# Layer 0 norms applied to the rows as they lie, and all clamps on GpSimd, in a bidirectional minGRU and ternary FFN kernel

## The chip, the cores and the metric

The kernel runs on one core of a Trainium2 chip. The metric is the device time of one execution in microseconds; of the kernel before there are three runs. A profiled execution gives a trace of every engine: TensorE (PE, with its weight loads as PEld), VectorE (DVE), ScalarE (ACT), GpSimd (POOL) and the sequencer that issues most transfers (SP).

## The reference, cut to what matters

`x` is 8 sequences of 512 tokens of 512 features. Each goes through a stack of four minGRU layers forwards and, reversed, backwards, with the same weights; the two results are fused by one linear layer and added to `x`, and a ternary feed-forward block follows.

```python
z = sigmoid(x @ Wz.T + bz);  h_tilde = tanh(x @ Wh.T + bh)
a = clip(1.0 - z, 1e-8, 1.0 - 1e-8)
h_t = a_t * h_(t-1) + z_t * h_tilde_t          # linear scan over the tokens
h = layernorm(h_new + (h if i > 0 else 0)) * gamma + beta    # over the features of a token
```

Here `Wz` is `Wh` and `bz` is `bh`, so a layer needs one matrix product. The forget factors `a` are clipped. A layer's norm needs mean and variance over the 512 features of each token.

## The kernel before, in words

Activations lie turned, with features on the 128 partitions (4 chunks of 128) and the 512 tokens along the free dimension, so that a scan over tokens is one VectorE instruction for a chunk. Sequences are worked in four pairs (0,1), (2,3), (4,5), (6,7); a state is a key `(b, d)` of sequence and direction. Layer 0 is shared by the two directions: one product for a chunk, two scans (`first_layer`, L523). For layers 1 to 3, `layer` (L579) runs the four states of the pair in turn.

Work is laid down in slots (`slot`, L464). A slot holds the four matmuls of one output chunk (`gates`, L482, or a chunk of `first_layer`), ScalarE's three activations (`factors`, L501: a, t, z), then on VectorE clamp, product, scan and residual, and between them pieces of earlier norms that two lists hand out: `turns` and `backs`. The slots are only a count, `now[0]`, at the time of writing: an item is taken when its due count is reached. The order on each engine is fixed by this program; engines meet by semaphores. Pools can hold an engine up: `ps_t` has 2 buffers (pt), `ps_u` 4, `tok` 10, `z` 16.

A norm (`norm`, L340) works by token tile. A turn transposes 128 tokens of the four chunks into a PSUM tile pt (L316), VectorE takes the statistics (`stats`, L168: bn_stats, bn_aggr, variance plus eps, minus mean), GpSimd the power -0.5 (L178), ScalarE writes the normalised token tile tok (L188, L189). When all four tok tiles stand, four back items transpose them to features again (pf, L325) and ScalarE writes `h * gamma + beta` chunk by chunk (L331). The norm of the last layer (`norm_last`, L354) takes only statistics, since its scale goes into the fusion; for the forward states of sequences 3, 5 and 7 ScalarE takes them in two passes over the tile (`two_passes`, L393: copy with a sum, square with a sum).

The norm of the input `x` is folded into layer 0: its weights are centred, and the product is multiplied by a tile `scale[b]` that holds each token's factor along the free dimension on all partitions. `scale_x` (L380) makes it by transposing a broadcast column on TensorE (L385) and copying it on ScalarE (L389).

The clamp of `a` is a VectorE instruction (L510) in all but the layer 0 chunks of sequences 0 and 1, where GpSimd makes it.

Layer 0 of the next pair is interleaved with the fusion of the pair before (L843 to L849): eight fusion tiles (two products, two VectorE steps L634, a store) and eight chunks; there VectorE also makes ternary weights (L193, L194), with loads and stores on SP. After that, layer 1 of the pair begins. All transfers in this stretch are issued by SP in program order.

Of the kernel before, what the change touches and what calls it, by code (L numbers as in the profile page):

```python
# [9 lines left out]
F32 = mybir.dt.float32  # L10
F32R = mybir.dt.float32r
AF = mybir.ActivationFunctionType
ALU = mybir.AluOpType
# [3 lines left out]
P = 128  # L17
LN_EPS = 1e-5
# [6 lines left out]
def kernel(  # L25
# [26 lines left out]
    nc = tc.nc  # L52
# [176 lines left out]
    with rec:  # L229
# [14 lines left out]
        class Tokens(list):  # L244
# [4 lines left out]
            def append(self, tile_):  # L249
                super().append(tile_)  # L250
                self.at = now[0] + self.lag

        def ready(at):
            if isinstance(at, Tokens):
                return len(at) == NT and at.at <= now[0]
            return at <= now[0] and held[0] < TOK

        def shares(cap):


            last = []
            for q in (turns, backs):
                some = []
                for i in range(max(2, cap)):
                    if not q or not ready(q[0][0]):
                        break
                    at, piece = q[0][:2]
                    late = (at.at if isinstance(at, Tokens) else at) + piece <= now[0]
# [71 lines left out]
        def norm(s, zs, tag, pause, pair=1):  # L340
# [10 lines left out]
            for c in range(NC_):  # L351
                queue(backs, s, toks, c // pair, back(toks, dst, c, True, f"{tag}_{c}"))

        def norm_last(s, tag):  # L354
            rsv[s] = small.tile([P, NT], F32, tag="rsv", name=f"rsv_{tag}")
            zs = [state[s][:, c, :] for c in range(NC_)]
            for t in range(NT):
                source, name = turned(zs, t, f"{tag}_{t}"), f"{tag}_{t}"
                queue(turns, s, now[0] + NC_ + 1, t, by_scalar(s, t, source, name) if s[0] > 1 and s[0] % 2 and s[1] == 0 else
                      tokens(source, None, rsv[s][:, t : t + 1], name))  # L360

        def by_scalar(s, t, source, name):
# [15 lines left out]
        rx, scale = {}, {}  # L378

        def scale_x(b):  # L380

            def go():
                pf = ps_f.tile([P, S], F32, tag="pf", name=f"pr_{b}")
                for t in range(NT):
                    nc.tensor.transpose(pf[:, ts(t, P)], rx[b][:, t : t + 1].broadcast_to([P, P]), ident)  # L385

                def last():
                    scale[b] = gp.tile([P, S], F32, tag="scale", bufs=2, name=f"scale_{b}")
                    nc.scalar.copy(scale[b], pf)  # L389
                return last  # L390
            return go
# [90 lines left out]
        def gates(h, l, o, name, scans):  # L482

            def work():
                u = ps_u.tile([P, S], F32, tag="u", name=f"u_{name}")
                for c in range(NC_):
                    nc.tensor.matmul(  # L487
                        u, lhsT=gw[l][:, c, ts(o, P)], rhs=h[:, c, :],
                        start=(c == 0), stop=(c == NC_ - 1),
                    )  # L490
                z = zp.tile([P, S], F32, tag="z", name=f"z_{name}")
                zlive[0] += 1
                a, t = factors(u, z, l, o, name)

                def end():
                    product(a, z, t)
                    scans(a, z)
                return end
            return work
# [9 lines left out]
        def clamp(engine, a):  # L509
            engine.tensor_scalar(a, a, CLAMP_HI, CLAMP_LO, ALU.min, ALU.max)  # L510

        def product(a, z, t, early=False):
            if not early:
                clamp(nc.vector, a)
            nc.vector.tensor_tensor(z, z, t, ALU.mult)  # L515

        def scan(dst, a, z, backward):
# [5 lines left out]
        def first_layer(b, lag=0):  # L523


            zf, zb = [], []

            def chunk(o):
                def work():
                    while zlive[0] + 2 > ZT:  # L530
                        slot(None, 2)
                    zlive[0] += 2
                    name = f"{b}_0_{o}"
                    u = ps_u.tile([P, S], F32, tag="u", name=f"u_{name}")
                    for c in range(NC_):
                        nc.tensor.matmul(  # L536
                            u, lhsT=gw[0][:, c, ts(o, P)], rhs=xT[b][:, c, :],
                            start=(c == 0), stop=(c == NC_ - 1),
                        )
                        if (b, o, c) in midway:  # L540
                            midway.pop((b, o, c))()

                    wait = 1 if (b, o) == (0, 0) else 0

                    def scaled():
                        z = zp.tile([P, S], F32, tag="z", name=f"z_{name}")
                        nc.vector.tensor_tensor(z, u, scale[b], ALU.mult)
                        a, t = factors(z, z, 0, o, name)

                        if b < 2:  # L550
                            stages.append((now[0], "clamps", lambda: clamp(nc.gpsimd, a)))
                        if wait:
                            for i, v in enumerate((bet, gam)):
                                nc.vector.tensor_copy(both[:, :, i, :], v.unsqueeze(2).broadcast_to([P, NC_, 64]))

                        def scans():
                            product(a, z, t, b < 2)
# [542 lines left out]
```

## Time and profile before

| | |
|---|---|
| median of 3 runs | 1714.09 us (1713.87 to 1714.39) |
| span of the profiled execution | 1711.6 us; its own time is not listed apart from this span, and the median stands 2.5 us above it |
| TensorE busy | 1701.2 us (99%) |
| VectorE busy | 1439.8 us (84%) |
| ScalarE busy | 1093.5 us (64%) |
| GpSimd busy | 222.5 us (13%) |
| granted TensorE clock | 1.000 |
| recurrent part | about 0 to 1240 us; feed-forward block behind it |

Times in the profile are microseconds from the first instruction. In a row of the timeline stand start, length, engine, line, operation, output and inputs; a bracket names how long the engine sat idle before and what ended that. Matmuls are pipelined, so a record is longer than the time that it adds: four transposes have a record of 0.60 us and the next row starts 0.43 or 0.44 us later. Records of VectorE overlap a little in the same way, and starts are the better measure. Layer 0 of the second pair lies at about 265 to 357 us, of the third at 561 to 656 us, of the fourth at 860 to 955 us. In the diff's count pairs begin with 1, so "pairs 2 to 4" are sequences 2 to 7.

### The profile page before, as it was taken

The page shows a single profiled execution, that of the slowest core. Times are in us where ns is not written, and L with a number is a line of the kernel's source. Part 1 is how long each engine was busy: PE and PEld are TensorE (multiplying, and loading weights), DVE is VectorE, ACT ScalarE, POOL GpSimd, SP SyncE. Part 2 cuts the span into 40 slices and gives each one's busy share as a digit, 9 for nine tenths or more (in the row PEclk, how much of TensorE's full clock was granted, in tenths as well). Part 3 has the DMA queues.
Part 4 walks back from the last instruction along what each step waited for, and adds up shares of the span by engine and source line. Part 5 has one row for each costly group of instructions (what it writes and reads, how often), then busy time and mean ns, then how long its engine had stood idle before and what let it go on. Part 6 is the DMA issues. An engine that isn't in the chain of part 4 may idle for free.

```text
span 1711.6 us, 19811 instructions
## 1 busy us (share of the span) xinstructions
PE 1701.2 (99%) x6440; PEld 1041.3 (61%) x6440; DVE 1439.8 (84%) x2835; ACT 1093.5 (64%) x1918; POOL 222.5 (13%) x342
## 2 busy tenths in 40 slices
PE   9999999999999999999999999999999999999999
PEld 5455554555555455555545555554688888888887
DVE  8999989889998888999888899995568768768877
ACT  6898873468886346888535688862356566666654
POOL 3111111111111111112111111110000000000000
PEclk9999999999999999999999999999999999999999
DMA  7002221150000125000012200102201101100100
GB/s 271 19 25 81 99 93 37 66 192 20 13 1 1 56 68 191 19 13 0 1 56 74 98 25 25 75 1 99 74 1 50 50 1 50 50 21 30 50 19 32
DMA packets 46599, 91.75 MB, mean 54 GB/s; under 512 B 5280, under 2 KB 5536, under 8 KB 45472
## 3 DMA queue, kind: packets, MB, share of 16 engines
q1 hardware_dynamic: 45488, 88.78, 15.2%
q10 hardware_dynamic: 1008, 1.70, 0.3%
q8 instruction: 51, 0.84, 0.2%
q14 instruction: 52, 0.43, 0.1%
HBM read 65.30 MB, written 25.17 MB: 53 GB/s over the span
## 4 chain that ended last, share of the span: by engine, by line
PE 86%; DVE 11%; ACT 2%; issue 1%; DMA 0%; POOL 0%; DVEq 0%; ACTq 0%
PE u L487 28%; PE po L939 14%; PE ph L912 14%; PE pu L624 13%; PE u L536 6%; PE pt L316 5%; PE pf L325 4%; DVE z L519 3%; DVE st L171 2%; DVE z L590 2%; DVE z L515 2%; PE py L214 1%; DVE a L510 1%; DVE mv L173 1%; ACT tok L189 0%
## 5 line engine op out<-in xcount | busy, mean ns | idle before, releaser
L487 PE MATMUL u<-xT,gw 128*128 128x512 f32 x768 | 345.5, 593 | 0.0
L487 PE MATMUL u<-h,gw 128*128 128x512 f32 x768 | 345.5, 592 | 0.0
L519 DVE TENSOR_TENSOR_SCAN z<-a,z 128x512 f32<-128x512 f32 x224 | 274.9, 1227 | 7.6
L487 PEld LDWEIGHTS u<-xT,gw 128*128 128x128 f32 x768 | 138.8, 190 | 138.7 <-issue 136.8
L487 PEld LDWEIGHTS u<-h,gw 128*128 128x128 f32 x768 | 138.6, 190 | 138.2 <-issue 138.0
L178 POOL TENSOR_TENSOR rs<-ve,mhalf 128x1 f32<-128x1 f32 x192 | 121.3, 632 | 672.7 <-DVE nmu L182 644.3
L939 PE MATMUL po<-pwq,ghi 128*128 128x512 f32 x512 | 202.8, 396 | 0.0
L939 PE MATMUL po<-pwq,glo 128*128 128x512 f32 x512 | 199.7, 390 | 0.0
L912 PE MATMUL ph<-yhi,fcq 128*128 128x512 f32 x512 | 199.7, 390 | 0.0
L504 ACT ACTIVATE a<-u,ngb 128x512 f32<-128x512 f32 x192 | 131.3, 684 | 107.0 <-PE u L487 106.3
L912 PE MATMUL ph<-ylo,fcq 128*128 128x512 f32 x512 | 199.4, 389 | 0.0
L916 ACT ACTIVATE g<-ph 128x512 f32<-128x512 f32 x128 | 76.4, 597 | 186.5 <-PE ph L912 186.5
L171 DVE BATCH_NORM_STATS2 st<-pt 128x6 f32<-128x512 f32 x244 | 168.6, 691 | 29.0 <-PE pt L316 28.8
L515 DVE TENSOR_TENSOR z<-z,t 128x512 f32<-128x512 f32 x224 | 153.5, 685 | 10.5 <-ACT z L506 10.5
L189 ACT ACTIVATE tok<-pt,nmr,rs 128x512 f32<-128x512 f32 x192 | 149.4, 778 | 6.4
L927 DVE TENSOR_TENSOR acc<-acc,g 128x512 f32<-128x512 f32 x112 | 77.3, 690 | 85.1 <-ACT g L916 84.2
L506 ACT ACTIVATE z<-u,gb 128x512 f32<-128x512 f32 x192 | 132.6, 691 | 0.0
L505 ACT ACTIVATE t<-u,gb 128x512 f32<-128x512 f32 x192 | 131.0, 682 | 0.0
L316 PEld LDWEIGHTS pt<-ident,z 128*128 128x128 f32 x640 | 78.6, 141 | 77.9 <-issue 55.5
L188 ACT ACTIVATE nmr<-nmu,rs 128x1 f32<-128x1 f32 x192 | 56.7, 295 | 106.9 <-POOL rs L178 95.5
L536 PE MATMUL u<-xT,gw 128*128 128x512 f32 x256 | 115.0, 593 | 0.8 <-DVE gw L769 0.8
L624 PE MATMUL pu<-fw,xT 128*128 128x512 f32 x256 | 115.2, 593 | 0.0
(165 smaller groups left out, 2646.3 us busy)
## 6 DMA issues: line engine op xcount, KB each, us to landing
xf<-in_x_dram SPq DMA_DIRECT2D x32, 256.0 KB, 5.5
x<-xf SPq DMA_DIRECT2D x32, 256.0 KB, 2.0
xy<-x SPq DMA_DIRECT2D x32, 256.0 KB, 4.3
xn<-in_x_dram SPq DMA_DIRECT2D x31, 256.0 KB, 4.3
out_dram<-xy SPq DMA_DIRECT2D x31, 256.0 KB, 2.0
xT<-in_xt_dram SPq DMA_DIRECT2D x7, 1024.0 KB, 7.5
fca<-in_fc_wT_dram SPq DMA_DIRECT2D x16, 256.0 KB, 2.9
pwa<-in_proj_wT_dram SPq DMA_DIRECT2D x16, 256.0 KB, 2.6
```

Of the source, the lines that this page charges most:

```text
L171: nc.vector.bn_stats(st, src)
L189: nc.scalar.activation(dst, src, AF.Identity, bias=nmr, scale=rs)
L316: nc.tensor.transpose(pt[:, ts(c, P)], zs[c][:, ts(t, P)], ident)
L487: nc.tensor.matmul(u, lhsT=gw[l][:, c, ts(o, P)], rhs=h[:, c, :], start=(c == 0), stop=(c == NC_ - 1),)
L504: nc.scalar.activation(a, u, AF.Sigmoid, bias=ngb[:, l, o : o + 1], scale=-1.0)
L506: nc.scalar.activation(z, u, AF.Sigmoid, bias=gb[:, l, o : o + 1])
L515: nc.vector.tensor_tensor(z, z, t, ALU.mult)
L519: nc.vector.tensor_tensor_scan(dst[:, d], a[:, d], z[:, d], 0.0, ALU.mult, ALU.add)
L536: nc.tensor.matmul(u, lhsT=gw[0][:, c, ts(o, P)], rhs=xT[b][:, c, :], start=(c == 0), stop=(c == NC_ - 1),)
L624: nc.tensor.matmul(pu, lhsT=hs[d][:, c, ts(t, P)], rhs=fw[:, d * NC_ + c, :], start=(c == 0), stop=(c == NC_ - 1),)
L912: nc.tensor.matmul(ph, lhsT=w, rhs=ys[b][c][i], start=(c == 0 and i == 0), stop=(c == NC_ - 1 and i == 1),)
L939: nc.tensor.matmul(po[b][t], lhsT=part[:, ts(t, P)], rhs=pwq[k // NP_][:, k % NP_, :], start=(k == 0 and i == 0), stop=(k == NF - 1 and i ...
```

## The change

For sequences 2 to 7 the norm of layer 0 is made by a new function, `norm_rows`. The turns stay: transposes into pt, statistics for each token tile, of tiles 0 and 1 by ScalarE in two passes, of tiles 2 and 3 by VectorE. Means and variances gather in a small tile pk; after the fourth tile one eps addition and one pow on GpSimd finish it. No tok tile is written and nothing is transposed back. Instead SP writes pk to DRAM as two rows of 512 numbers, and two further transfers spread each row over 128 partitions into two [128, 512] tiles. VectorE then subtracts the one from and multiplies the other into each chunk as it lies, and ScalarE applies gamma and beta to the result. These applications are due two slots after the rows were asked for.

The tile `scale[b]` of sequences 2 to 7 is spread by transfers in the same way. The last norm of the forward states of sequences 2, 4 and 6 also goes to ScalarE's two passes. Every clamp of `a` is given to GpSimd. For the first of each pair, turns and backs of layer 0 are handed out one a slot, for the second two a slot.

```diff
+        def spread(dst, i, row):
+            nc.sync.dma_start(out=dst, in_=row[i : i + 1, :].broadcast_to([P, S]))
+
+        def norm_rows(s, zs, tag, pause, pair=1):
+            rows_, at = Rows(), now[0] + pause
+            pk = small.tile([P, 2, NT], F32, tag="pk", bufs=6, name=f"pk_{tag}")
+            wide = []
+            def close():
+                nc.vector.tensor_scalar(pk[:, 1, :], pk[:, 1, :], LN_EPS, None, ALU.add)
+                nc.gpsimd.tensor_tensor(pk[:, 1, :], pk[:, 1, :], mhalf.broadcast_to([P, NT]), ALU.pow)
+                row = dram.tile([2, S], F32, tag=f"row_{tag}", name=f"row_{tag}")
+                nc.sync.dma_start(out=row.rearrange("i (t p) -> p i t", p=P), in_=pk)
+                for i in range(2):
+                    wide.append(tokp.tile([P, S], F32, tag="tok", name=f"wide{i}_{tag}"))
+                    spread(wide[i], i, row)
+                rows_.at = now[0] + 2
+            def turn(t):
+                source, name = turned(zs, t, f"{tag}_{t}"), f"{tag}_{t}"
+                def go():
+                    src = source()
...
+                    if t >= 2:
+                        st = small.tile([P, 6], F32, tag="st", name=f"st_{name}")
+                        nc.vector.bn_stats(st, src)
+                        nc.vector.bn_aggr(pk[:, :, t], st)
+                        if t == NT - 1:
+                            close()
+                        return lambda: None
+                    def last():
+                        sm, ss = (small.tile([P, 1], F32, tag=k, name=f"{k}_{name}") for k in ("sm", "ss"))
+                        mean, var = pk[:, 0, t : t + 1], pk[:, 1, t : t + 1]
+                        nc.scalar.activation(src, src, AF.Copy, accum_out=sm)
+                        nc.scalar.activation(mean, sm, AF.Copy, scale=1.0 / H)
+                        nc.scalar.activation(src, src, AF.Square, bias=mean, scale=-1.0, accum_out=ss)
+                        nc.scalar.activation(var, ss, AF.Copy, scale=1.0 / H)
+                    return last
+                return go
+            def apply(c):
+                def go():
+                    nc.vector.tensor_tensor(zs[c], zs[c], wide[0], ALU.subtract)
+                    nc.vector.tensor_tensor(zs[c], zs[c], wide[1], ALU.mult)
...
+                    def last():
...
+                        nc.scalar.activation(
+                            state[s][:, c, :], zs[c], AF.Identity,
+                            bias=bet[:, c : c + 1], scale=gam[:, c : c + 1],
+                        )
+                    return last
+                return go
+            for t in range(NT):
+                queue(turns, s, at, t // pair, turn(t))
+            for c in range(NC_):
+                queue(backs, s, rows_, c // pair, apply(c))
...
         def norm_last(s, tag):
...
-                queue(turns, s, now[0] + NC_ + 1, t, by_scalar(s, t, source, name) if s[0] > 1 and s[0] % 2 and s[1] == 0 else
+                queue(turns, s, now[0] + NC_ + 1, t, by_scalar(s, t, source, name) if s[0] > 1 and s[1] == 0 else
...
         def scale_x(b):
+            def spread_x():
+                row = dram.tile([1, S], F32, tag=f"rowx_{b}", name=f"rowx_{b}")
+                nc.sync.dma_start(out=row.rearrange("i (t p) -> p (i t)", p=P), in_=rx[b])
+                scale[b] = gp.tile([P, S], F32, tag="scale", bufs=2, name=f"scale_{b}")
+                spread(scale[b], 0, row)
+            if b > 1:
+                return spread_x
...
                 a, t = factors(u, z, l, o, name)
+                clamp(nc.gpsimd, a)
...
-        def product(a, z, t, early=False):
-            if not early:
-                clamp(nc.vector, a)
+        def product(z, t):
             nc.vector.tensor_tensor(z, z, t, ALU.mult)
...
-                        if b < 2:
-                            stages.append((now[0], "clamps", lambda: clamp(nc.gpsimd, a)))
+                        stages.append((now[0], "clamps", lambda: clamp(nc.gpsimd, a)))
...
-                                norm((b, 0), zf, f"{b}0_0", 2 if b == 1 else 1, 2 if b < 2 else 1)
+                                (norm if b < 2 else norm_rows)((b, 0), zf, f"{b}0_0", 2 if b == 1 else 1, 2 if b < 2 or b % 2 else 1)
...
-                                    norm((b, 1), zb, f"{b}1_0", 2 if b == 1 else 1, 2 if b < 2 else 1)
+                                    (norm if b < 2 else norm_rows)((b, 1), zb, f"{b}1_0", 2 if b == 1 else 1, 2 if b < 2 or b % 2 else 1)
```

More of the change, by code (lines that the diff above doesn't have):

```diff
@@ L251, in append @@
                 self.at = now[0] + self.lag
+        class Rows:
+            at = None
         def ready(at):
+            if isinstance(at, Rows):
+                return at.at is not None and at.at <= now[0]
             if isinstance(at, Tokens):
@@ L267, in shares @@
                     at, piece = q[0][:2]
-                    late = (at.at if isinstance(at, Tokens) else at) + piece <= now[0]
+                    late = (at.at if isinstance(at, (Tokens, Rows)) else at) + piece <= now[0]
                     if i >= cap and not late:
@@ L352, in norm @@
                 queue(backs, s, toks, c // pair, back(toks, dst, c, True, f"{tag}_{c}"))
+        def spread(dst, i, row):
[17 more added lines that the diff above has]
+                    src = source()
+                    if t == 0:
+                        held[0] += 2
+                    if t >= 2:
[18 more added lines that the diff above has]
+                    nc.vector.tensor_tensor(zs[c], zs[c], wide[1], ALU.mult)
+                    zlive[0] -= 1
+                    if c == NC_ - 1:
+                        held[0] -= 2
+                    def last():
+                        if s not in state:
+                            state[s] = hp.tile([P, NC_, S], F32, tag="h", name=f"h_{s[0]}{s[1]}")
+                        nc.scalar.activation(
[8 more added lines that the diff above has]
+                queue(backs, s, rows_, c // pair, apply(c))
@@ L493, in work @@
                 a, t = factors(u, z, l, o, name)
+                clamp(nc.gpsimd, a)
                 def end():
-                    product(a, z, t)
+                    product(z, t)
                     scans(a, z)
@@ L556, in scans @@
                         def scans():
-                            product(a, z, t, b < 2)
+                            product(z, t)
                             f = zp.tile([P, S], F32, tag="z", name=f"zf_{name}")
```

## The prediction

> **What bounds the kernel now.** I read the busy table first, then the windows of the stages that the change touches, then TensorE's and VectorE's rows in time through one layer 0 to layer 1 passage, and last the rows where GpSimd clamps already run.
>
> ```profile
> PE 1701.2 (99%) x6440; PEld 1041.3 (61%) x6440; DVE 1439.8 (84%) x2835; ACT 1093.5 (64%) x1918; POOL 222.5 (13%) x342
> ...
> 561.00:656.00 95.00, 95.00 (x302) 47.72 (x301) 80.09 (x148) 38.06 (x71) 11.29 (x17) 1.00 0.26 84
> 656.00:735.00 79.00, 78.76 (x291) 42.60 (x290) 73.13 (x161) 65.36 (x112) 14.30 (x23) 1.00 0.23 80
> ```
>
> In the windows the columns after the length are PE, PEld, DVE, ACT and POOL. TensorE never pauses, so only fewer matmuls or transposes can save time. But from 656 on, where layer 1 of a pair begins, VectorE is 93% busy: it is a second bound close behind.
>
> ```profile
> 690.93 0.69 DVE L171 BATCH_NORM_STATS2 st<-pt 128x6 f32<-128x512 f32 x1
> 691.66 0.18 DVE L173 BATCH_NORM_AGGREGATE mv<-st 128x2 f32<-128x6 f32 x1
> 691.95 0.15 DVE L177 TENSOR_SCALAR ve<-mv 128x1 f32<-128x1 f32 x1
> 692.02 0.14 DVE L182 TENSOR_SCALAR nmu<-mv 128x1 f32<-128x1 f32 x1
> 692.08 0.42 DVE L510 TENSOR_SCALAR a<-a 128x512 f32<-128x512 f32 x1
> 692.42 0.68 DVE L515 TENSOR_TENSOR z<-z,t 128x512 f32<-128x512 f32 x1
> 693.13 1.22 DVE L519 TENSOR_TENSOR_SCAN z<-a,z 128x512 f32<-128x512 f32 x1
> 694.39 0.69 DVE L590 TENSOR_TENSOR z<-z,h 128x512 f32<-128x512 f32 x1
> ```
>
> One VectorE slot. Records overlap, so I price by start to start: bn_stats 0.73, aggregate 0.29, each small 0.065, clamp 0.33, product 0.72, scan 1.25, residual 0.61: 4.07 us with the next start, against 4.31 us of TensorE (3.44 of matmuls and two groups of four transposes, 0.43 each).
>
> ```profile
> 635.47 3.60 PE L536 MATMUL u<-xT,gw 128*128 128x512 f32 x8
> ...
> 668.16 0.66 PE L316 MATMUL pt<-ident,z 128*128 128x128 f32 x4 [0.24 <-ACT tok L189]
> ...
> 698.81 0.60 PE L325 MATMUL pf<-ident,tok 128*128 128x128 f32 x4
> ```
>
> From the last layer 0 chunk of the pair (635.47) to the first transposes back of layer 1's first norm (698.81) TensorE takes 63.34 us, with one wait of 0.24. The second end is a hard link: those transposes need the last of four token tiles.
>
> ```profile
> 696.16 0.15 DVE L177 TENSOR_SCALAR ve<-mv 128x1 f32<-128x1 f32 x1
> ...
> 697.48 0.78 ACT L189 ACTIVATE tok<-pt,nmr,rs 128x512 f32<-128x512 f32 x1
> ```
>
> That tile ended at 698.26, 2.1 us after VectorE's eps addition and 0.55 before TensorE wanted it. VectorE can fall behind here by half a microsecond before TensorE waits.
>
> **The change, part by part.**
>
> *TensorE.* Per pair from the second on 4 x 16 transposes back and 2 x 4 of the scale go: 72 x 0.109 = 7.85 us, in all 23.5 us. With nothing else in the way the span becomes 1688.1. Of each 7.85 us, 52 transposes (5.7 us) lie between the two rows above, and 20 (2.2 us) outside.
>
> *VectorE in that stretch.* Counted in the order of instructions from the multiplication by the scale in the pair's last chunk to that eps addition. Before: 13 bn_stats, 13 aggregates, 24 small, 9 clamps, 9 products, 10 scans, 8 residuals, 5 ternary pairs (0.515 + 0.67), 4 fusion steps (0.75), 2 bias additions (0.60), the multiplication (0.65): 52.4 us. The trace has 57.2 us there, of which 4.4 are waits (1.58, 1.50, 0.92, 0.40): 56.8, so the prices hold. After: 4 bn_stats, 4 aggregates, 14 small and 9 clamps fewer (8 us less), and 14 subtractions and 14 multiplications by the spread tiles more. These read two SBUF tiles as product and residual do: 0.73 (its partner waits for it) and 0.61, 18.8 us. Sum 63.2 us.
>
> Ahead of it stand one statistic, its eps addition and two such pairs (3.8), and two fusion steps (1.5), so it starts 5.3 us after TensorE begins that chunk. With the tail of 2.1 the end cannot come before 5.3 + 63.2 + 2.1 = 70.6 us: 7.3 later than today's 63.3, although TensorE alone would need 57.6. Net of the 2.2 saved outside: **+5.1 us per pair, a floor.**
>
> *ScalarE's order.* ScalarE now takes the statistics of tiles 0 and 1 in two passes (0.58 + 0.19 + 0.20 + 0.66 + 0.19: 1.83 us each). For the norm of (b+1, forward) they stand behind the affines of two chunks that wait for VectorE, which reaches them 24.3 us into the stretch; TensorE wants the two pt buffers back at 21.5. They come free at 26.2 and 28.1, so TensorE waits and VectorE, next in need of tiles 2 and 3, idles 0.8 and 0.9. With a like knot later: +2.2 (0 to 4).
>
> *GpSimd clamps.* 216 go from VectorE (0.33 us of occupancy each) to GpSimd.
>
> ```profile
> 21.74 1.23 DVE L519 TENSOR_TENSOR_SCAN zf<-a,z 128x512 f32<-128x512 f32 x1
> 22.88 1.56 DVE L519 TENSOR_TENSOR_SCAN z<-a,z 128x512 f32<-128x512 f32 x1
> ...
> 22.13 1.24 POOL L510 TENSOR_SCALAR a<-a 128x512 f32<-128x512 f32 x1
> ```
>
> A clamp takes 0.61 alone (the shortest of 8); beside a scan it takes 1.24, and the scan behind it 1.56 instead of 1.23. So a clamp that falls among two-input operations gives its 0.33 back. The Trainium skill, "SBUF — State Buffer", section "SBUF: two separate sides", says that the two engines share a port pair by an exclusive lock for a whole instruction. By that rule a scan would be held up to 0.61, nearly twice the clamp's saving, and 10 clamps would cost 6.1 us per pair; the row is what I sum by. In the stretch 10 clamps, and 78% of VectorE's time is two-input work: 10 x 0.33 x 0.78 = 2.6 us (0 to 3.3). In steady slots it costs nothing: 3.74 + 0.33 is still below 4.31. GpSimd's pows now queue behind a clamp; its idle time covers that. Where VectorE's clamps go in layers 2 and 3 nothing is gained, since TensorE is full there.
>
> *The round trip by DMA.* SP waits for the pow, writes 1024 single elements, waits, and spreads two tiles of 256 KB. No row shows such a write. Below: a 256 KB store, 2.0 us. Above: 1024 packets at 91 ns (15.2% of 16 engines' span over 45488 packets) on 16 engines, 5.8, plus that 2.0. The spreads: 3.8 (3.4 for one, 0.4 for the second issue), issues 0.7. Together 6.5 to 12.3; between, as its packets are many but tiny: 9.5. VectorE's own order leaves 10.9, 13, 8.6 and 9.9 us for the four norms of a pair, so 0.9 is exposed once: +1 (0 to 5.3). The skill's "DMA: Bandwidth & Descriptors", section "Rules for kernel authors", says a strided last dimension becomes one descriptor per element and should be rearranged, which speaks against this write. Its fixed cost of about 2 us each would make the trip some 5 us and hide all of it (estimate from that page). SP's later stores and loads stand behind the wait for the row; their users come 5 us or more later. The scale's own trip starts slots ahead.
>
> *Elsewhere.* Three more last norms on ScalarE (12 x 1.83) fit in its idle third. TensorE's short waits for tok in pair 1 (2.5 us in 7) may shrink: -1. The last pair has no x statistic (1.1 us) in the stretch.
>
> **Sum**: 3 x (5.1 + 2.2 + 2.6 + 1.0) - 1.1 - 1 = +30.6 on the span of 1711.6: 1742. The median of the runs (1714.1) lies 2.5 above that span: **1744 us**, 1.8% slower.
>
> **The rivals.**
> 1. *VectorE's lag is absorbed* and TensorE stays full: 1714.1 - 23.5 = 1691. For it: over the whole program VectorE has some 65 us less (clamps 90.6, 36 statistics of 1.15, against 96 new operations of 0.69). Against: the token tile has 0.55 us of slack in the trace, not 13. It decides if those pairs of operations take under 0.8 us instead of 1.34.
> 2. *The DMA round trip dominates*, 16 us or more: 5.1, 7.4 and later knots per pair come on top, 1775 or beyond. For it: element writes; against: queues nearly empty there.
> 3. *Clamps cost VectorE 0.45 or more in steady slots*, which then pass TensorE's 4.31 where x statistics (1.10) fall: some 0.6 us in each of 30 groups of four slots, +19: 1763.
> 4. *Gains and knots cancel*: 1714, if floor and knots come to 0.
>
> **How the numbers follow.** My case 0.80, rival 1 0.05, rival 2 0.06, rival 3 0.06, rival 4 0.03. 0.2% is about what a measurement of this kernel can tell from no change; so faster 0.05, same 0.03, slower 0.92. Range: the floor alone gives 3 x 5.1 - 2.1 = +13, 1727, and a little cheaper operations 1724; all upper ends, 3 x (5.1 + 4 + 3.3 + 5.3) - 2, give +51, 1765, and part of rival 3 1768.
>
> **What would show it.** In the profile after: TensorE idle of 10 us or more at each start of layer 1, ended by tok or by ScalarE's reading of pt, and full elsewhere; VectorE at 95% or more there without long waits; few scans at 1.56; the row's landing between 2 and 8 us. I am wrong if TensorE is full through layer 1, or if VectorE's new operations wait long for the spread tiles.

## The result, and the profile after

The changed kernel takes **1794.63 us** (median of 4 runs, 1790.64 to 1796.46), beside 1714.24 us (4 runs) of the kernel before: **1.0467 times as long, 95% interval 1.0454 to 1.0479**. The prediction was 1744 us, 1724 to 1768: right about slower, far short in size. The profiled execution took 1790.64 us, with a span of 1788.8; spans differ by 77.2 us.

The page of the kernel after: busy time, the granted TensorE clock over 40 equal slices, and the chain of work that ended last, by engine and by line.

```profile
span 1788.8 us, 19434 instructions
...
PE 1701.7 (95%) x6224; PEld 1026.7 (57%) x6224; DVE 1416.8 (79%) x2559; ACT 1103.2 (62%) x2020; POOL 369.5 (21%) x522
...
PEclk9999999989999998899999899999999999999999
...
PE 75%; DVE 10%; DMA 8%; ACT 4%; POOL 1%; issue 1%; SPq 0%; DVEq 0%; ACTq 0%
PE u L573 26%; PE po L1023 13%; PE ph L996 13%; PE pu L708 9%; PE u L621 5%; DMA row<-pk 5%; PE pt L323 5%; PE pf L332 3%; DVE z L604 2%; DMA wide<-row 2%; DVE z L600 1%; DVE st L171 1%; DVE z L674 1%; DMA wq_pw<-pwq 1%; DVE z L411 1%
```

TensorE is busy as long as before (1701.7 against 1701.2 us), but idles 87.1 us instead of 10.4. That it is busy as long hides two things: 216 transposes are gone (23.5 us), and the records of the other matmuls are about 24 us longer, while the granted clock, 1.000 before, now dips three times. `row<-pk` and `wide<-row`, the row's write and its two spreads, are 7% of the chain.

Two windows of the kernel after, which answer to the two shown of before (after the length: PE, PEld, DVE, ACT, POOL, each with its instructions; then the granted clock, the DMA share, GB/s).

```profile
561.00:661.00 100.00, 100.00 (x307) 49.35 (x306) 79.12 (x125) 49.64 (x110) 22.76 (x32) 1.00 0.12 35
661.00:751.00 90.00, 67.39 (x175) 31.58 (x173) 68.52 (x113) 40.94 (x77) 15.44 (x18) 0.87 0.42 137
```

The first is full as it was. All of the loss lies in the second, the passage from layer 0 to layer 1: TensorE 67.4 of 90 us, and VectorE, 93% busy there before, now 76%. VectorE was meant to be the bound, yet it waits. From here on a *passage* is, as in the prediction, the time from TensorE's last layer 0 chunk to its first transposes back of layer 1's first norm. It took 63.3, 63.3 and 63.7 us into pairs 2, 3 and 4; now 90.6, 89.4 and 87.5. The growth sums to 77.2 us, the whole difference of the spans.

What VectorE waited for, in the passage into pair 3 (timeline, VectorE; the bracket holds the idle time before the row and what ended it):

```profile
665.53 0.69 DVE L410 TENSOR_TENSOR zf<-zf,wide 128x512 f32<-128x512 f32 x1 [3.33 <-DMA wide<-row]
667.23 0.69 DVE L411 TENSOR_TENSOR zf<-zf,wide 128x512 f32<-128x512 f32 x1 [1.01 <-DMA wide<-row]
...
714.39 0.69 DVE L410 TENSOR_TENSOR zf<-zf,wide 128x512 f32<-128x512 f32 x1 [4.53 <-DMA wide<-row]
...
728.62 0.69 DVE L411 TENSOR_TENSOR z<-z,wide 128x512 f32<-128x512 f32 x1 [2.16 <-DMA wide<-row]
```

Four waits, 11.0 us. The timeline of SP in the same kernel says why:

```profile
700.14 0.38 SPq L376 DMA_DIRECT2D row<-pk  x1
711.17 0.80 SPq L363 DMA_DIRECT2D wide<-row  x2
712.08 0.37 SPq L376 DMA_DIRECT2D row<-pk  x1
722.23 2.14 SPq L363 DMA_DIRECT2D wide<-row  x2
```

From the issue of a row's write to SP's next instruction, the spread, pass 11.0 and 10.2 us: SP waits for the row to land. The second norm's row stands behind the first norm's in SP's queue. Over the twelve norms (listing of the transfers: KB each, median us to landing):

```profile
wide<-row SPq DMA_DIRECT2D x24, 256.0 KB, 5.0
...
row<-pk SPq DMA_DIRECT2D x12, 4.0 KB, 10.4
```

4 KB take twice as long as 256 KB. The page counts 16128 more packets under 512 bytes than before. But moving them is not what takes the time. Two windows of the same kernel, behind the row issued at 700.14, with the DMA engines' share in the last column but one:

```profile
701.00:702.00 1.00, 1.00 (x4) 0.52 (x3) 0.97 (x2) 0.00 (x0) 0.00 (x0) 1.00 0.47 4
702.00:711.00 9.00, 8.22 (x32) 4.35 (x30) 5.16 (x9) 7.15 (x18) 2.25 (x3) 1.00 0.00 0
```

The packets move within 2 us of the issue; then the DMA engines stand idle (0.00) for 9 us until SP goes on at 711.17. What those 9 us consist of is not shown. And what TensorE made of it (timeline, TensorE):

```profile
660.78 3.60 PE L621 MATMUL u<-xT,gw 128*128 128x512 f32 x8
...
694.41 1.12 PE L323 MATMUL pt<-ident,zf 128*128 128x128 f32 x4 [7.70 <-ACT pt L402]
...
697.20 5.24 PE L573 MATMUL u<-xT,gw 128*128 128x512 f32 x8
...
725.62 0.47 PE L323 MATMUL pt<-ident,z 128*128 128x128 f32 x1 [5.21 <-DVE z L674]
725.89 6.25 PE L573 MATMUL u<-h,gw 128*128 128x512 f32 x8
...
750.20 0.49 PE L332 MATMUL pf<-ident,tok 128*128 128x128 f32 x3
```

None of these waits names the DMA. Between them stands ScalarE (its timeline):

```profile
690.57 0.81 ACT L419 ACTIVATE h<-z,bet,gam 128x512 f32<-128x512 f32 x1 [7.49 <-DVE z L411]
```

The late application holds ScalarE's affine (L419), which holds its two passes over pt (L402) behind it, which hold TensorE's next transposes: 7.70 us. Behind the waits stand groups of 5.24 and 6.25 us that take 3.60 elsewhere.

### The profile page after: what moved, and what is told of

It reads as the page before. It is cut to its first block, busy times and chain, and to the rows that moved or that the text cites. A ratio compares the mean times of both kernels' runs of the same rounds, so it can differ in the third digit from the quotient of the medians.

```text
span 1788.8 us, 19434 instructions
## 1 busy us (share of the span) xinstructions
PE 1701.7 (95%) x6224; PEld 1026.7 (57%) x6224; DVE 1416.8 (79%) x2559; ACT 1103.2 (62%) x2020; POOL 369.5 (21%) x522
## 4 chain that ended last, share of the span: by engine, by line
PE 75%; DVE 10%; DMA 8%; ACT 4%; POOL 1%; issue 1%; SPq 0%; DVEq 0%; ACTq 0%
PE u L573 26%; PE po L1023 13%; PE ph L996 13%; PE pu L708 9%; PE u L621 5%; DMA row<-pk 5%; PE pt L323 5%; PE pf L332 3%; DVE z L604 2%; DMA wide<-row 2%; DVE z L600 1%; DVE st L171 1%; DVE z L674 1%; DMA wq_pw<-pwq 1%; DVE z L411 1%
## 5 line engine op out<-in xcount | busy, mean ns | idle before, releaser
L573 PE MATMUL u<-xT,gw 128*128 128x512 f32 x768 | 352.7, 603 | 5.4 <-DVE xf L718 5.4
L573 PE MATMUL u<-h,gw 128*128 128x512 f32 x768 | 352.4, 603 | 0.0
L597 POOL TENSOR_SCALAR a<-a 128x512 f32<-128x512 f32 x224 | 155.5, 694 | 699.8 <-ACT a L591 698.9
L573 PEld LDWEIGHTS u<-h,gw 128*128 128x128 f32 x768 | 142.3, 195 | 145.8 <-issue 145.8
L1000 ACT ACTIVATE g<-ph 128x512 f32<-128x512 f32 x128 | 76.4, 597 | 186.3 <-PE ph L996 186.3
L171 DVE BATCH_NORM_STATS2 st<-pt 128x6 f32<-128x512 f32 x184 | 127.7, 694 | 25.5 <-PE pt L323 19.1
L1011 DVE TENSOR_TENSOR acc<-acc,g 128x512 f32<-128x512 f32 x112 | 77.3, 690 | 84.9 <-ACT g L1000 84.0
L323 PE MATMUL pt<-ident,z 128*128 128x128 f32 x640 | 97.7, 276 | 32.7 <-DVE z L674 22.5
L708 PE MATMUL pu<-fw,h 128*128 128x512 f32 x256 | 117.1, 601 | 6.0 <-DVE xf L718 6.0
L621 PE MATMUL u<-xT,gw 128*128 128x512 f32 x256 | 115.0, 593 | 1.1 <-DVE gw L853 0.8
```

The source lines that it names most:

```text
L171: nc.vector.bn_stats(st, src)
L323: nc.tensor.transpose(pt[:, ts(c, P)], zs[c][:, ts(t, P)], ident)
L573: nc.tensor.matmul(u, lhsT=gw[l][:, c, ts(o, P)], rhs=h[:, c, :], start=(c == 0), stop=(c == NC_ - 1),)
L621: nc.tensor.matmul(u, lhsT=gw[0][:, c, ts(o, P)], rhs=xT[b][:, c, :], start=(c == 0), stop=(c == NC_ - 1),)
L708: nc.tensor.matmul(pu, lhsT=hs[d][:, c, ts(t, P)], rhs=fw[:, d * NC_ + c, :], start=(c == 0), stop=(c == NC_ - 1),)
```

## The experiments

The expectations name theories by letters: A, the row's write makes the trip long; V, VectorE's amount of work in the passage; C, contention by GpSimd's clamps; K and Q, ScalarE's order; H, the clock. Times are medians; the ratio is to the kernel before on the same chip. Passages are into pairs 2, 3 and 4.

| kernel | us | ratio, 95% interval | passages, us |
|---|---|---|---|
| after | 1794.6 | 1.0467 (1.0454 to 1.0479) | 90.6, 89.4, 87.5 |
| clamps_only | 1712.5 | 0.9994 (0.9984 to 1.0003) | |
| scale_only | 1710.6 | 0.9984 (0.9974 to 0.9993) | |
| scale_clamps | 1710.3 | 0.9981 (0.9972 to 0.9989) | 63.5, 63.5, 63.5 |
| norms_only | 1798.2 | 1.0496 (1.0480 to 1.0512) | 91.3, 90.0, 89.3 |
| short_row | 1755.6 | 1.0242 (1.0225 to 1.0259) | 78.1, 75.8, 78.2 |
| row_by_transpose | 1753.8 | 1.0237 (1.0220 to 1.0254) | 77.3, 76.5, 75.0 |
| no_subtract | 1721.7 | 1.0045 (1.0029 to 1.0060) | 65.5, 65.0, 62.1 |
| stats_vector | 1749.2 | 1.0204 (1.0189 to 1.0219) | 74.2, 74.0, 72.9 |
| affine_pool | 1761.0 | 1.0272 (1.0258 to 1.0286) | 78.6, 78.2, 76.4 |
| fill | 1815.3 | 1.0593 (1.0577 to 1.0608) | 98.5, 97.1, 97.7 |
| fill_half | 1796.7 | 1.0490 (1.0471 to 1.0510) | 91.2, 91.4, 87.4 |
| fwd_rows | 1726.6 | 1.0077 (1.0063 to 1.0091) | 70.3, 70.7, 69.4 |
| even_rows | 1738.8 | 1.0146 (1.0132 to 1.0160) | 74.2, 75.1, 73.5 |
| fwd_pairs | 1722.9 | 1.0050 (1.0038 to 1.0063) | 70.2, 68.6, 68.6 |
| fwd_pool | 1726.9 | 1.0071 (1.0058 to 1.0085) | 71.1, 69.4, 70.5 |
| scale_clamps_moved | 1722.9 | 1.0054 (1.0041 to 1.0067) | 63.5, 63.5, 63.5 |
| fwd_moved | 1717.3 | 1.0020 (1.0011 to 1.0029) | 62.8, 62.8, 62.8 |
| rows_moved | 1743.5 | 1.0175 (1.0159 to 1.0190) | 69.1, 68.9, 67.8 |

### The parts apart

**clamps_only**, the kernel before with

```diff
                 a, t = factors(u, z, l, o, name)
+                clamp(nc.gpsimd, a)
...
-            if not early:
-                clamp(nc.vector, a)
```

> The kernel before, with the clamps of all layers on GpSimd and nothing else changed. Theory A (the prediction's term for GpSimd's clamps: 2.6 us per passage while VectorE is short, nothing in steady slots): here VectorE loses 216 clamps of 0.33 us and gets at most that back, TensorE stays full, so 1711 to 1717 us. Rival C (contention between GpSimd's clamps and VectorE's scans is what made the changed kernel slow): the clamps alone must cost a good part of the 80 us, so 1735 us or more.

1712.5 us: inside A's band, C is out. **scale_only**, the kernel before with `spread_x` for sequences 2 to 7 and the wider use of the two passes:

```diff
+            if b > 1:
+                return spread_x
...
-  by_scalar(...) if s[0] > 1 and s[0] % 2 and s[1] == 0 else
+  by_scalar(...) if s[0] > 1 and s[1] == 0 else
```

> The kernel before, with only the scale of pairs 2 to 4 spread by DMA and ScalarE's two passes for all last norms of (b, forward). Theory A: 24 transposes of 0.109 us go from a full TensorE, and the scale's trip (landings of 8.4 and 4.6 us in the changed kernel) starts slots ahead of its use: 1711.5 us (1709 to 1715). Rival: ScalarE's 12 more double passes or the trip hold TensorE up: 1718 us or more.

1710.6 us, 3.0 less where 2.6 was worked out. **scale_clamps** is both.

> The two parts that did no harm, together: the kernel before with the scale of pairs 2 to 4 by DMA (-3.0 us alone) and all clamps on GpSimd (-1.1 alone), its norms as they were. Theory A: the two add, as they touch different engines: 1709.5 us (1708 to 1711.5). Rival: no more than the scale alone gives, 1710.6.

1710.3 us. It is below both kernels; that it beats the scale alone (1710.6) can't be told. **norms_only** is the changed kernel with the clamps back on VectorE (the clamp's diff reversed).

> The changed kernel with the clamps of layers 1 to 3, and of layer 0 from pair 2 on, back on VectorE. Theory A: what is lost is lost in the three norms' passages whoever clamps. VectorE gets 10 clamps of 0.33 us back per passage and is rid of at most 2.6 us of contention, so 1790 to 1805 us. Rival C (GpSimd's clamps hold VectorE up): 1770 us or less.

1798.2 us, as A says: undoing the clamps cost some 4 us, about as much as the changed kernel's own runs differ (5.8), and the passages grew by 0.7, 0.6 and 1.8 us. So all of the loss belongs to the norms by rows.

### The row's write

**short_row**:

```diff
-   row = dram.tile([2, S], ...)
-   nc.sync.dma_start(out=row.rearrange("i (t p) -> p i t", p=P), in_=pk)
+   row = rows4[turn4[0] % 4]            # four rows, filled with ones at the start
+   nc.sync.dma_start(out=row[0:1, 0 : 2 * NT], in_=pk[0:1].rearrange("p i t -> p (i t)"))
```

> The changed kernel, but of each norm's 1024 means and scales only the 8 of partition 0 are written, as one run of 32 bytes, into a row of DRAM that was filled with ones at the start; all waits stay, the spread tiles are still read back from that row, and what they hold is not the norm's. Theory A (the write of 1024 single elements, 10.4 us to landing, is what made VectorE, ScalarE and then TensorE late): the row lands in 2 to 4 us, each trip is 7 us shorter, and what remains is VectorE's own work: 1735 to 1755 us. Rival V (VectorE's 28 new operations per passage are the cause, and the trip lies beside them): 1780 us or more. Rival P (the norms cost nothing but the trip): 1700 us or less.

1755.6 us: 39 us less, 0.6 outside A's upper end, and far from V's and P's. Its timeline of SP, in the same passage:

```profile
650.41 0.23 SPq L382 DMA_DIRECT2D row<-pk  x1
651.51 0.80 SPq L368 DMA_DIRECT2D wide<-row  x2
```

1.1 us where 10.2 to 11.0 stood, and VectorE waits for no spread tile in that passage. **row_by_transpose** keeps the values and drops the single elements:

```diff
+   pf = ps_f.tile([P, S], F32, tag="pf", name=f"pk_t_{tag}")
+   nc.tensor.transpose(pf[0 : 2 * NT, 0:P], pk.rearrange("p i t -> p (i t)"), ident)
+   nc.scalar.copy(wide[1][0 : 2 * NT, 0:P], pf[0 : 2 * NT, 0:P])
-   nc.sync.dma_start(out=row.rearrange("i (t p) -> p i t", p=P), in_=pk)
+   nc.sync.dma_start(out=row.rearrange("i (t p) -> (i t) p", p=P), in_=wide[1][0 : 2 * NT, 0:P])
```

> The changed kernel, whose output stays the reference's, but pk (128 partitions of 8 values) is turned by one transpose in the slot after its statistics, copied out of PSUM by ScalarE, and written as 8 runs of 512 bytes instead of 1024 of 4; the applications start three slots after the last statistics instead of two. Theory A (the single-element write is the trip's excess): the row lands in 2 to 4 us, and the time comes near the short row's 1755.6: 1750 to 1765 us. Rival: the wait for a slot, the transpose and the copy give back what the write saves, 1780 us or more.

1753.8 us. SP's rows there:

```profile
642.74 0.28 SPq L383 DMA_DIRECT2D row<-wide  x1
643.99 0.80 SPq L363 DMA_DIRECT2D wide<-row  x2
```

The same 4 KB as 8 runs of 512 bytes: 1.25 us here, 1.2 to 1.6 over the twelve norms, instead of about 10.5. Two different edits agree that the single-element write is worth 39 to 41 of the 80 us. Some 40 us remain, with a short trip.

### What remains: VectorE's work, or the order?

**no_subtract** is the short-row kernel without the line `nc.vector.tensor_tensor(zs[c], zs[c], wide[0], ALU.subtract)`.

> The short-row kernel (only 8 of each norm's 1024 values written, the rest of the row being ones) with VectorE's subtraction of the spread mean left out of all twelve norms; the multiplication stays. Theory V (with a short trip VectorE's own work sets the end of each passage, now 78.1, 75.8 and 78.2 us long): 14 subtractions of 0.7 us per passage go, 9.8 us, so 1755.6 - 29 = 1726 us (1718 to 1736). Rival T (the remaining fixed time of the trip sets it): 1750 us or more, since the trip is the same.

1721.7 us, within V's band. The medians differ by 33.9 us, 11.3 a passage, for 9.8 us of work (the profiled execution was the fastest of five, and its passages are 13.2 us shorter on average). **stats_vector** is the short-row kernel with one condition changed, so ScalarE takes no statistics:

```diff
-                    if t >= 2:
+                    if t >= 0:
```

> The short-row kernel with the statistics of tiles 0 and 1 of the row norms on VectorE too (bn_stats and aggregate), none in two passes on ScalarE. Theory V (VectorE bounds the passage; the knot of ScalarE's order and the two PSUM tiles pt costs little, 2.2 us as predicted): VectorE gets 8.2 us more per passage and loses some 4 us of waits for those tiles, so 1765 to 1775 us. Rival K (the knot decides: TensorE waits 8.7 us per passage for ScalarE's reading of pt): those waits go and the time falls to 1745 us or less.

1749.2 us, between the two: VectorE had more to do and yet the passages became 3.7 us shorter. The extra work in the passage was less than the 8.2 us expected: into pair 3 the passage holds 116 VectorE instructions instead of 108, so four statistics and not eight (69.4 us busy instead of 66.5). The knot at ScalarE's two passes is real and larger than the 2.2 us given to it. With it gone VectorE is busy for 94% of that passage (69.4 of 74.0 us), so what then bounds it is VectorE.

**fwd_rows** and **even_rows** shrink the change to one or two of the four norms of a pair, with the short trip:

```diff
-  (norm if b < 2 else norm_rows)((b, 0), zf, ...)
+  (norm if b < 2 or b % 2 else norm_rows)((b, 0), zf, ...)
-  (norm if b < 2 else norm_rows)((b, 1), zb, ...)      # fwd_rows alone
+  norm((b, 1), zb, ...)
```

> The scale and the clamps as in the changed kernel, but only the forward norm of the first sequence of pairs 2 to 4 by rows, with the row written through a transpose; the three other norms of a pair as before. Theory V (a passage is as long as the larger of TensorE's and VectorE's work in it): VectorE gets 8 new operations of 0.67 us, 5.4 us, and loses 10 clamps and two tiles' statistics, some 5.5 us, so it stays where it was and TensorE saves 15 transposes of 0.109 us per pair: 1709.5 - 4.9 = 1704.6 us (1702 to 1708). Rival (any affine behind VectorE holds ScalarE's queue and with it TensorE): 1712 us or more.

> As the forward-only kernel, with both norms of the first sequence of pairs 2 to 4 by rows. Theory V: VectorE gets 16 new operations, 10.7 us, and loses some 8 us, so it ends some 3 us after TensorE in each passage, where TensorE saves 30 transposes, 3.3 us: about even with the two harmless parts alone, 1704 to 1713 us. Rival (the passage is held by each affine behind VectorE): 1718 us or more.

1726.6 and 1738.8 us: both miss V's number, fwd_rows by 22 us. Theory V as I had counted it, over the whole passage, fails here. The timeline of fwd_rows, ScalarE's rows, shows the affine of the fourth chunk:

```profile
663.81 0.81 ACT L426 ACTIVATE xT<-zf,bet,gam 128x512 f32<-128x512 f32 x1 [9.88 <-DVE zf L418]
```

and TensorE's rows its wait for that affine:

```profile
664.68 2.07 PE L580 MATMUL u<-xT,gw 128*128 128x512 f32 x2 [5.31 <-ACT xT L426]
```

VectorE applied that chunk some 11 us after the third one, behind fusion and ternary work. That spoke for the order (Q), and three more runs tried it: affines on GpSimd (**affine_pool**, on row_by_transpose), two applications per slot (**fwd_pairs**, on fwd_rows), and both (**fwd_pool**).

```diff
-   nc.scalar.activation(state[s][:, c, :], zs[c], AF.Identity, bias=bet[...], scale=gam[...])
+   nc.gpsimd.tensor_scalar(state[s][:, c, :], zs[c], gam[...], bet[...], ALU.mult, ALU.add)
```
```diff
-                queue(backs, s, rows_, c // pair, apply(c))
+                queue(backs, s, rows_, c // 2, apply(c))
```

> The kernel with the row written through a transpose (1753.8 us), with the affine of the applied chunks (times gamma, plus beta) on GpSimd instead of ScalarE. Theory Q (ScalarE works in order: an affine that waits for VectorE's late application holds back the two passes and the reads of pt behind it, and so TensorE): ScalarE's long waits go and TensorE's waits for its reading of pt with them, 1725 to 1742 us. Theory V (the amount of VectorE's work alone sets each passage): VectorE's work is the same, so 1747 us or more.

> The forward-only kernel (1726.6 us) with its four applications two per slot instead of one, so the fourth stands ahead of VectorE's ternary work and its waits instead of behind. Theory Q (in the forward-only kernel VectorE had time enough: only the place of the fourth application, 12 us behind the third, held ScalarE for 9.9 us and TensorE for 5.3): 1704 to 1711 us. Theory V (its amount of work): 1722 us or more.

> As the run with two applications per slot, and the affine of those chunks on GpSimd. Theory Q: nothing is left of the waits behind the affines, 1703 to 1709 us. Theory V: 1722 us or more. Where GpSimd's affine holds up its pows for the token norms, 1712 us or more.

1761.0, 1722.9 and 1726.9 us, none within Q's band. Moving the fourth application forward gave 3.7 us, and that is the cleanest of the three. The affine on GpSimd made it worse, but it was not only a change of order: in affine_pool VectorE is busy for 71.7 us of each passage instead of 66.3, and into pair 3 six of its ten scans take 1.61 us instead of 1.23, beside GpSimd's affines. In fwd_pairs the next late thing took the place at once (timeline, TensorE):

```profile
664.06 0.66 PE L323 MATMUL pt<-ident,zf 128*128 128x128 f32 x4 [3.82 <-ACT tok L189]
...
665.82 4.89 PE L580 MATMUL u<-xT,gw 128*128 128x512 f32 x8
```

That tok waits for statistics which VectorE reaches at 661.13. Windows of 23 us, of fwd_pairs just before that:

```profile
641.00:664.00 23.00, 19.24 (x57) 9.11 (x55) 20.53 (x36) 8.10 (x13) 2.04 (x3) 1.00 0.46 150
```

and of scale_clamps, which differs only in the norms, at the same stage, which it reaches some 4 us earlier:

```profile
637.00:660.00 23.00, 23.00 (x79) 12.03 (x78) 17.30 (x33) 9.57 (x15) 2.76 (x5) 1.00 0.50 161
```

20.5 instead of 17.3 us of VectorE. My sum for fwd_rows had credited it with statistics saved before 620 and clamps most of which are saved from 660 on; in these 23 us, where fusion, ternary work and applications meet, it gains work.

The last three runs test that by taking *other* VectorE work out: the weights' ternary pairs go to layers 2 and 3 of pairs 2 and 3, in the harmless kernel (control), in fwd_pairs and in row_by_transpose.

```diff
-                    pieces((1, 2, 1, 0, 1, 2, 2, 3)[t + (b % 2) * NT])
+                    if b >= B - 2:
+                        pieces((1, 2, 1, 0, 1, 2, 2, 3)[t + (b % 2) * NT])
...
                 slot(gates(h, l, o, f"{s[0]}{s[1]}_{l}_{o}", scans))
+                if 2 <= s[0] < B - 2 and l >= 2 and o % 2:
+                    pieces(1)
```

> Control for the two runs beside it. The two harmless parts together (1710.3 us), with the 32 pieces of the weights' quantisation (their ternary pairs on VectorE) moved from the fusions of pairs 1 to 3, that is out of the passages, to every other slot of layers 2 and 3 of pairs 2 and 3, where TensorE is full and VectorE has half a microsecond per slot left. The norms are those of the kernel before and TensorE waits for nothing in these passages, so both theories expect 1709 to 1712 us.

> The forward-only kernel with two applications per slot (1722.9 us), with the same move of the quantisation. The norm's work, the trip, the affines and the order of everything else are as they were. Theory V (the amount of VectorE's work just ahead of layer 1 decides: 5 ternary pairs of 1.19 us and a wait of 1.5 for their DMA go from the passage): TensorE's wait of 3.8 us and the slow matmuls behind it go, and its 15 transposes per pair are saved at last: 1703 to 1709 us. Theory Q (order and trip): 1718 us or more.

> The kernel with all norms by rows, the row written through a transpose (1753.8 us), with the same move. Theory V: each passage (77.3, 76.5 and 75.0 us) loses 6.0 us of ternary pairs and 1.3 of their wait: 1726 to 1737 us. Theory Q: 1747 us or more.

1722.9, 1717.3 and 1743.5 us. All three miss their absolute numbers, since the move itself costs 12.5 us in layers 2 and 3: VectorE had less room there than I gave it, and the list of TensorE's waits in the control names the place:

```profile
PE pf L325 <- ACT tok L189: 11.1, 9, 1.8
```

(us in all, times, longest; 1.0 us in the kernel without the move). But the control's passages stay at 63.5 us, and so the passages can be compared. With the move, the forward norm by rows makes a passage of 62.8 us, with one wait of TensorE of 0.2 us into pair 3, and the run is 5.6 us faster than its control; 45 transposes at 0.109 us are 4.9. Without the move the same norm cost 12.6 us (1722.9 against 1710.3). With all norms by rows a passage loses 7.7 us, 7.3 expected. So it is the amount of VectorE's work ahead of layer 1; its order was worth 3.7 us in fwd_pairs. One thing is not separated: with the ternary pairs go their loads and stores on SP, and VectorE's wait for one of them (1.49 us in fwd_pairs).

### The clock

**fill** and **fill_half** put matmuls that nobody reads into TensorE's waits:

```diff
+   junk = ps_f.tile([P, S], F32, tag="pf", name=f"junk_{name}")
+   for i in range(n):                   # fill: 16 and 12; fill_half: 8 and 5
+       nc.tensor.matmul(junk, lhsT=ident, rhs=fw[:, i % NC_, :], start=True, stop=True)
```

> The changed kernel with extra matmuls (identity by fusion weights, 128x512, into a PSUM tile that nobody reads; the output is the reference's) in TensorE's order at the two longest waits of each of the three passages: 16 ahead of the transposes of the third token tile of the (b+1, forward) norm, where TensorE waits 7.7 us for ScalarE, and 12 ahead of the first transposes of layer 1's first norm, where it then waits 5.2 us for VectorE: 84 matmuls, 36 us of work more. Theory H (after such a wait TensorE runs at about half its clock for some microseconds: eight matmuls take 5.24, 6.25 and 6.00 us there instead of 3.60; work in the wait keeps the clock up): the slow groups go, up to 5.3 us per passage, and since VectorE bounds part of it, the time falls by 4 to 16 us, to 1779 to 1791 us. Rival (the clock has another cause, or the slow matmuls lie beside the late engines anyway): 1794 us or more.

> As the fill kernel, with 8 and 5 matmuls instead of 16 and 12. Those were sized wrong: one such matmul takes 0.86 us (13.90 us for 16), so they came to 24 us per passage where the waits were 13, and TensorE was late by its own filler (the passages grew from 89 to 98 us) although every group behind them ran at full rate. Now 6.9 and 4.3 us per passage lie inside the waits of 7.7 and 5.2. Theory H (the lower clock after the waits is a cost of its own): the slow groups (5.24, 6.25) go back to 3.60, 4 us per passage, of which part lies beside late engines: 1782 to 1791 us. Rival (VectorE and the trip set the end, and TensorE's lower clock lies beside them): 1792 to 1797 us, the time of the changed kernel.

1815.3 us for fill, whose filler was twice too long, and 1796.7 for fill_half, no better than the changed kernel. Rows of fill_half (TensorE):

```profile
690.08 7.03 PE L356 MATMUL junk<-fw,ident 128*128 128x512 f32 x16
...
700.66 3.60 PE L584 MATMUL u<-xT,gw 128*128 128x512 f32 x8
...
729.39 0.33 PE L329 MATMUL pt<-ident,z 128*128 128x128 f32 x1 [4.03 <-DVE z L685]
729.56 5.29 PE L584 MATMUL u<-h,gw 128*128 128x512 f32 x8
```

Where the wait was filled, the group behind it is back at 3.60 us; the second wait was not (4.03 us left), and its group stays slow. So work in the wait keeps the rate up there. But the passages (91.2, 91.4, 87.4 us) did not shrink: TensorE only waited a little longer for the late engines. In this kernel the lower clock, where the filler undid it, lies beside the cause and added nothing that shows; the waits that were not filled stay open. What it costs where TensorE alone bounds was not tried.

## Why the prediction was wrong in size, step by step

**What bounds the kernel; the place** (a second bound close behind TensorE, in the passage): right. All of the 77.2 us lie there.

**TensorE** (23.5 us less of transposes): the work is gone, but none of it came out as time. The 2.2 us per pair expected outside the passage went into what follows it; in short_row, into pair 3, TensorE waits 2.56 us there for a tok, and a group behind it takes 6.47 us. That also corrects the link at the end of the passage: there, and in the rows above (750.20, x3), three of the first four transposes back run ahead, and only the fourth waits for the last token tile.

**VectorE's floor, ScalarE's knot and the clamps** (63.34 + 7.3 + 2.2 + 2.6 = 75.4 us per passage without the trip): short_row has 78.1, 75.8 and 78.2, mean 77.4, and row_by_transpose 76.3, so the mechanism holds, and the size within 2 us a passage. Part of that closeness is luck, since the terms inside are off both ways. The knot was too small: stats_vector gained 3.7 us although VectorE got four statistics more. The clamps were too dear: into pair 3 the changed kernel shows four residual additions of 0.91 or 0.92 us instead of 0.69 and one bias addition of 1.10 instead of 0.68, some 1.3 us where 2.6 were summed; with the clamps on VectorE (norms_only) none of these is longer than 0.69. No scan is held in that passage (1.23 us), and over the whole program the mean scan moved only from 1.227 to 1.237 us. The Trainium skill, "SBUF — State Buffer", section "SBUF: two separate sides", has one engine hold the port pair for a whole instruction. Delays of 0.2 to 0.4 us beside clamps of 0.61 us agree with that, but they were fewer than its rule would allow.

**The round trip by DMA** (9.5 us, 6.5 to 12.3; exposed +1, 0 to 5.3 per pair): **this is the step that failed.** From the issue of the row to the use of both spread tiles pass 15 to 17 us (651.19 to 667.23, 700.14 to 715.13, 712.08 to 728.62). The write, bounded by 2.0 and 7.8 us, takes 10.2 to 11.0 in that passage. It lays 11.8 us onto each (89.2 against 77.4), where 1 was summed. (By the four slacks listed there, a trip of 12.3 us would have exposed up to 7.5, not 5.3; that too falls short.) The upper bound was no bound, because it priced the packets, at 91 ns each, and took a 256 KB store's 2.0 us for the rest. In the trace it is the rest that takes the time: of the row issued at 700.14 the packets have moved within 2 us, and the 9 us behind them were in no term. The Trainium skill, "DMA: Bandwidth & Descriptors", section "Rules for kernel authors", had it the right way: a strided last dimension becomes a descriptor per element and should be rearranged. The trace agrees (1.25 us once rearranged). The estimate of a 5 us trip that I drew from that page's fixed cost, which the page fits on transfers issued by GpSimd and not by SP, was wrong for this write: only the rearranged trip comes near it.

**Elsewhere** (-1 in pair 1, -1.1 in the last): the first was not seen; scale_clamps idles 11.2 us of TensorE, before 10.4. The second shows in part: the last passage is the shortest in the changed kernel, row_by_transpose and stats_vector (by 1.1 to 3.1 us), but not in short_row.

**The sum without the trip.** 1744 less the 3 us for the trip is 1741; the two kernels with a short trip took 1754 and 1756. So some 13 to 15 us more were missing: 1 to 2 us in each passage, the 2.2 us per pair outside that did not come, and most of the 2 us under "elsewhere". By themselves they would have stayed within the range; the write is what took the time out of it.

**The rivals.** The one that came true is the second, a DMA round trip that dominates, with 1775 us or beyond, held at 0.06, though it came together with my own terms. Of the list of what would show the prediction wrong, the long waits for the spread tiles are what the trace shows. VectorE at 95% without waits was wrong too: 76% in the changed kernel, and 88% (66.5 of 75.8 us) with the short row; only without ScalarE's two passes as well does it come to 94%.

## What to carry to other kernels

A transfer whose writes are single elements has to be priced from a row of the same kind or be rearranged: one small transpose and copy turned 10.5 us into 1.3. Moving work from a full TensorE to VectorE paid here only where VectorE had room in that very stretch of some 20 us; a balance over a longer stretch counted savings that lay elsewhere. And when an order looks guilty, take other work out of the same engine before reordering: the next late item stood right behind.

## What the runs showed of the hardware

- A 4 KB row written as 1024 elements of 4 bytes landed after 10.4 us (median of 12, 8.5 to 12.2); 512 elements took 8.4 in the same run and 8.8 in scale_clamps, 10.8 in short_row, so the time does not follow the number of elements. Of one such write the packets moved within 2 us of its issue, and 9 us passed with the DMA engines idle before it counted as landed. As 8 runs of 512 bytes it took 1.2 to 1.6 us, and one run of 32 bytes 1.1.
- TensorE's granted clock, 1.000 all through before, fell to 0.981 over the span, 0.87 in one passage: groups of eight matmul records took up to 6.25 us instead of 3.60 behind waits. The Trainium skill, "TensorE: Matmul & The Clock Gate", Part 1, tells of half the clock after an idle window of about 3.4 us, until as long a busy one has passed. The trace agrees after 7.70 and 5.21 us of waiting: in the first of these the granted clock is 1.00 up to 690, some 3 us into the wait, and 0.50 from 692 to 700. After shorter waits it went both ways: 5.40 us behind a wait of 1.94 in fill_half, 3.70 behind 2.16 in the changed kernel.
- With GpSimd's affine beside VectorE (affine_pool, into pair 3), six of ten scans took 1.61 us instead of 1.23, and VectorE was busy 5 us longer in the passage.
- Keeping the clock up in the longest wait of each passage brought no time back (1796.7 against 1794.6 us), as other engines were late there anyway.
